# Key features by column blocks, token normalising in SBUF by GpSimd, and a reordered end, in a kernel of convolution, attention and experts

## The chip, the cores and the metric

The kernel runs on one core of a Trainium2 chip. The metric is the device time of one execution in microseconds (us). The core's engines are TensorE (PE in the profile; PEld is its loading of weights), VectorE (DVE), ScalarE (ACT), GpSimd (POOL) and SyncE (SP), which issues all DMAs of this kernel from one queue in program order. Engines run side by side and wait for each other by semaphores. All data is float32, and each matmul stands in the profile as two records.

## The reference, cut to what matters

Eight images of 128 channels and 36 x 36 positions go through two layers. The names of the inputs are shortened here.

```python
# layer 0: group norm, convolutions, an attention of 1296 queries on 34*34 keys, 1x1 convolutions
x = x + _L0_conv_ref(_gn(x), c0, w_x, ...)
# layer 1, on tokens: t is (8, 1296, 128)
t = _to_tokens(x)
t = t + _L1_attn_ref(_ln_t(t), ...)
t = t + _L1_ffn_ref(_ln_t(t), ...)

def _L1_attn_ref(x, mask, Wq, bq, Wk, bk, w, bw):
    q = einsum('bld,ed->ble', x, Wq) + bq
    k = einsum('bld,ed->ble', x, Wk) + bk
    t = tanh(q[:, :, None, :] + k[:, None, :, :])
    scores = einsum('bijd,d->bij', t, w) + bw[0]
    return einsum('bij,bjd->bid', softmax(scores), x)

def _L1_ffn_ref(x, gate_w, gate_b, weight1, weight2):   # 64 experts, the 8 best tokens of each
    probs = softmax(einsum('bsd,ed->bse', x, gate_w) + gate_b, axis=1)
    topv, topi = the 8 largest over s, for each expert
    pooled = einsum('bked,bke->bed', x at topi, topv)
    h = gelu([pooled, 1] @ weight1)          # 129 x 512 for each expert
    out = [h, 1] @ weight2                   # 513 x 128 for each expert
    return zeros with out * topv added at topi
```

The tanh of a sum, for all 1296 x 1296 pairs and 128 channels of each image, is nearly all of the work.

## The kernel before

**Scores.** The sum over 128 channels of w * tanh(q + k) is turned into quotients of sums over products: 8 blocks (`NF`) of 128 features are made of each query (`qf`, exponentials of `a_q` times the tokens) and of each key (`kf`, of `a_k`). For each slot PE makes denominators `d` and numerators `n` out of `qf` and `kf` (`products`, L903 to 916), ACT makes 1/d as exp(-ln d) (`lq`, L933 and L936), and the products n * lq are added up. In slots k = 2, 5, 8, 11 (`DVE_PAIRS`) DVE multiplies and adds (L951 to 960); in the other slots DVE multiplies into `rp` (L964, three buffers) and POOL adds (`accp`, L971 and L973). ACT takes the exponential `e` of the sum (L993). A unit is one chunk of 432 queries against one tile of 128 keys and has 12 slots; the last tile of an image has 16 keys, comes sixth (`order`, L879) and takes 2 slots. An image has 3 chunks of 11 units, and the loop of L1072 goes through all slots of all images. `denominators` runs three slots ahead of `numerators`.

**What runs beside the scores.** Everything else is written as generators in four lanes (L1026), highest first: `first_of_all` (query features, the small tile's sums), `urgent` (`attend`: softmax-weighted sum of tokens, once the 11 `e` of a chunk are there), `gates` (`gating` of the image before) and `background` (of the next image: `normal`, `conv_keys`, `layer0`, `tokens`, `keys`). Each generator yields what it wants next. `take_turns` (L1031) runs steps that want no matmul, at most one for each lane in a slot, and in a slot of `DVE_PAIRS` for `first_of_all` only. `matmul_turn` (L1036) runs a turn of matmuls after each slot's own; `background` and the others are paced by a balance that grows by 400 columns per slot (`PACE`), and get no turn in the slot before one of `DVE_PAIRS`. So the order of all engines' instructions is fixed when the program is built.

**Steps that the change touches.** `tokens` (L586) transposes the image by PE (`tpl`) to `tok`, writes that to DRAM, takes mean and variance by DVE, transposes the image a second time (`tpn`), and DVE normalises from PSUM into `xh` (L640); `xh` is transposed to `xT`. `keys` (L664) makes the key features of one tile of 128 keys in two turns of four matmuls; ACT takes one exponential of 128 x 512 for each turn (L684), and SP writes to `kd` in DRAM. `prefetch` (L887) loads a unit's features `kf` from there two units ahead. For the 16-key tile POOL writes two masked copies (L689). `attend` works through each chunk's four query tiles with 11 matmuls in two PSUM groups. `gate_logits` transposes attended tokens `t2` to `t2T`, stores that to DRAM as the residual `t2d`, transposes it back (`tp3`), and DVE normalises from PSUM (L800). `gate_tokens` takes the softmax and the 8 largest for each expert, writes them to DRAM (`gd`) and makes `pooled`.

**The end.** After the loop the score buffers are given up. Four groups of expert weights (`load_experts`: 4 experts, w1 and w2 of 1 MB each, 4 buffers for each) are loaded, the last chunk's `attend` and the last image's gating run, then SP issues all gates and residuals, and 16 groups run: `inner` (matmuls with w1, bias, gelu), `turned` (transposes) and `outer` (matmuls with w2). The loads of group 4 and on are issued in that loop. Results go through DRAM (`eod`), are multiplied by the gates, added to the residuals and written out.

Of the kernel before, what the change touches and what calls it, by code (L numbers as in the profile page):

```python
# [70 lines left out]
def kernel(  # L71
# [44 lines left out]
    kd = [dram.tile([NKT, 128, NF * 128], F32, tag=f"kd{b % 2}", name=f"kd{b}") for b in range(NB)]  # L116
# [4 lines left out]
    pooled = const.tile([128, E, NB], F32, tag="pooled", name="pooled")  # L121
# [5 lines left out]
    with ExitStack() as loop, ExitStack() as score:  # L127
# [7 lines left out]
        big = pool("big", 8, ctx)  # L135
        chunks = pool("chunks", 8)
        etp = pool("etp", NKT + 1)
# [131 lines left out]
        TAKE = (False, 1)  # L269

# [313 lines left out]
        prepared, made = {}, set()  # L584

        def tokens(b):  # L586
# [43 lines left out]
            yield matmuls(3)  # L630
            for g in range(0, NKT, 2):
                tp = aux("tpn")
                some = list(range(g, min(g + 2, NKT)))
                for t in some:
                    o, n = KT[t]
                    turned_to(tp[:n, (t - g) * C : (t - g + 1) * C], r[:, o : o + n], ident)
                yield TAKE
                for t in some:
                    n = KT[t][1]
                    nc.vector.tensor_scalar(  # L640
                        xh[:n, t, :C], tp[:n, (t - g) * C : (t - g + 1) * C],
                        mv[:n, t, 0:1], rs[:n, t : t + 1], ALU.subtract, ALU.mult,
                    )
                yield matmuls()
# [19 lines left out]
        def keys(b, tiles):  # L664

            xT = prepared[b][1]
            yield matmuls(1)
            for t in tiles:
                o, n = KT[t]
                first = (b, t) == (0, order[0])  # L670
                if first:
                    kf_of[0] = kfp.tile([128, NF, 128], F32, tag="kf", name="kf")
                for q0 in (0, NF // 2):
                    some = slice(q0, q0 + NF // 2)
                    pk = aux("pk1").rearrange("p (q t) -> p q t", t=128)
                    for q in range(NF // 2):
                        bmm(pk[:, q, :n], a_k[:, (q0 + q) * 128 : (q0 + q + 1) * 128],
                           xT[:, o : o + n], start=True, stop=True)
                    yield TAKE
                    if first:  # L680
                        ks = kf_of[0][:, some, :]
                    else:
                        ks = kstp.tile([128, NF // 2, 128], F32, tag="ks", name="ks")
                    nc.scalar.activation(ks[:, :, :n], pk[:, :, :n], AF.Exp)  # L684
                    kd3 = kd[b][t].rearrange("p (q t) -> p q t", t=128)[:, some, :]
                    if n == REM:

                        for x in range(2):
                            nc.gpsimd.tensor_scalar(  # L689
                                ks[:, :, (x + 1) * n : (x + 2) * n], ks[:, :, :n],  # L690
                                pairs[:, min(q0, 1), x : x + 1], None, ALU.mult,
                            )
                        nc.sync.dma_start(kd3[:, :, : 2 * n], ks[:, :, n : 3 * n])
                    else:
                        nc.sync.dma_start(kd3, ks)
                    if q0 > 0:
                        made.add((b, t))
                    yield matmuls()
# [15 lines left out]

        def attend(b, c, es):
# [11 lines left out]
            for i, at in enumerate(own):  # L727
                sums = two.tile([T, C + 1], F32, tag="sums", name="sums")
                for some in (range(6), range(6, NKT)):
                    pa = aux("pa1")[:T, : C + 1]  # L730
                    for j in some:
                        if j < NKT - 1:
                            e, v = es[j][:, i * T : (i + 1) * T], xh[:, j, :]
                        else:
                            rows = slice(32 * i, 32 * i + REM)
                            e, v = es[j][rows, :T], xr[rows]
                        bmm(pa, e, v, start=(j == some[0]), stop=(j == some[-1]))
                    yield TAKE
                    if j < NKT - 1:
                        nc.vector.tensor_copy(sums, pa)  # L740
                        yield matmuls()
# [21 lines left out]
        def gate_logits(b, chunks):  # L763
# [23 lines left out]
            for c in chunks:  # L787
                tp, tt = turned(c, "t2T")
                yield TAKE
                nc.vector.tensor_copy(tt, tp[:, :CH])  # L790
                nc.sync.dma_start(t2d[b][:, c * CH : (c + 1) * CH], tt)
                yield matmuls(1)
                for j0 in range(0, TPC, 2):
                    tp = aux("tp3")
                    for j in (j0, j0 + 1):
                        turned_to(tp[:T, j * C : (j + 1) * C], tt[:, j * T : (j + 1) * T], ident)
                    yield TAKE
                    for j in (j0, j0 + 1):
                        t = c * TPC + j
                        nc.vector.tensor_scalar(  # L800
                            t2[:T, t, :], tp[:T, j * C : (j + 1) * C],
                            mv[:, t, 0:1], rs[:, t - tiles[0] : t - tiles[0] + 1],
                            ALU.subtract, ALU.mult,
                        )
                    yield matmuls()
# [65 lines left out]

        def drain(*gens):
            for g in gens:
                for _ in g:
                    pass
# [11 lines left out]
        def prefetch(u):  # L887
            if u < len(units) and u not in kf_of:
# [3 lines left out]
                kf = kfp.tile([128, NF, 128], F32, tag="kf", name="kf")  # L892
                nc.sync.dma_start(
                    kf[:, :, :n], kd[b][j].rearrange("p (q t) -> p q t", t=128)[:, :, :n]
# [92 lines left out]
        def exps(p, u, d):  # L987
# [6 lines left out]
            es.setdefault((b, c), {})[j] = e  # L994
            if len(es[b, c]) == NKT:
                urgent.append(attend(b, c, es.pop((b, c))))
# [34 lines left out]
        def take_turns(p, k):  # L1031
            for lane in lanes:
                if lane.due(p, False) and (k not in DVE_PAIRS or lane is first_of_all):
                    lane.run(p)
# [25 lines left out]
        drain(tokens(0), keys(0, order[:1]))  # L1060
# [7 lines left out]
        drain(keys(0, order[1:3]))  # L1068
        prefetch(1)
        urgent.append(keys(0, order[3:]))  # L1070
        pending = deque()
        for p, (u, k) in enumerate(slots):  # L1072
            b, c, j = units[u]
            rem = j == NKT - 1
            if k == 0:
                prefetch(u + 2)
                if c == 0 and j == 1:
                    if b > 0:
                        gates.append(gating(b - 1))
                    if b + 1 < NB:  # L1080
                        background.extend(
                            (normal(b + 1), conv_keys(b + 1), layer0(b + 1), tokens(b + 1),
                             keys(b + 1, range(NKT)))
# [20 lines left out]
        while pending:  # L1104
# [7 lines left out]
            tc.tile_pool(name="wts", bufs=4, side="right", reuse_waits="tile")  # L1112
# [7 lines left out]
        def load_experts(g):  # L1120
            es = slice(g * EG, (g + 1) * EG)
            w1 = wts.tile([128, EG, HID], F32, tag="w1", name="w1")
            nc.sync.dma_start(w1, weight1[es, :128, :].rearrange("e d h -> d e h"))
# [168 lines left out]
```

## Time and profile before

| what | us |
|---|---|
| median of three runs | 6157.78 |
| lowest and highest run | 6153.82, 6159.6 |
| the profiled execution | 6152.63 |
| its span, first to last instruction | 6150.6 |
| first `e` of the scores (L993) starts | 199.5 |
| last `e` starts | 5978.4 |
| first matmul of the experts (L1165) | 6016.5 |
| last copy to `out_s` ends | 6119.8 |

Of the page, the busy shares say how long each engine had an instruction in it, the row PEclk the clock that TensorE was granted in tenths, the row GB/s what DMA moved in each of 40 slices. Granted clock of the core over the span: 0.986. In a group's line the number behind the bar is the busy time, then the mean duration of one instruction in ns, then the idle time of the engine just before them with what ended it. In views by stretch of time, busy times of each engine are given in us with the number of instructions. A chain of waits goes back from the last instruction, at each step to what released it; "issue" is time for which the profile shows no wait.

### The profile page before, as it was taken

Reading aid. Unit: us, or ns where it says so; the run is one execution under the profiler, and the core shown is the slowest. Engines: PE = TensorE matmul, PEld = TensorE weight load, DVE = VectorE, ACT = ScalarE, POOL = GpSimd, SP = SyncE. Lnnn points to the kernel's source line nnn. Section 1 sums busy time; section 2 is a strip of 40 time slices with the busy share of each in tenths; the row PEclk is TensorE's granted clock in tenths of the full one; section 3 lists DMA queues with packets and bytes.
Section 4 is the critical chain, followed back from the end, with each engine's and each line's share of the span. In section 5 each row is a group of like instructions: output and inputs, shape, how many; then the busy total and the mean of one; then the engine's idle time right before and its main releaser. Section 6 shows DMA issues by size and latency. Waiting matters only on the chain.

```text
span 6150.6 us, 93223 instructions
## 1 busy us (share of the span) xinstructions
PE 5963.4 (97%) x33576; PEld 2866.4 (47%) x33576; DVE 4798.4 (78%) x9518; ACT 5281.1 (86%) x5371; POOL 4597.5 (75%) x2804
## 2 busy tenths in 40 slices
PE   7999999999999999999999999999999999999996
PEld 5454444544544445444445444454454444544443
DVE  4787878878787787877888777887778878788872
ACT  1888898888988899888998899888898888999980
POOL 4777777777778777878687777877777777787870
PEclk9999999999999999999999999999999999999997
DMA  1200011000210001100111001100021000100017
GB/s 47 71 33 22 25 62 52 20 25 28 72 38 24 26 32 64 42 22 23 49 52 37 22 20 63 45 33 22 28 71 39 24 26 27 61 29 29 25 71 262
DMA packets 150239, 270.88 MB, mean 44 GB/s; under 512 B 45392, under 2 KB 74960, under 8 KB 149776
## 3 DMA queue, kind: packets, MB, share of 16 engines
q1 hardware_dynamic: 149776, 264.92, 12.9%
q8 instruction: 265, 4.34, 0.3%
q14 instruction: 198, 1.62, 0.1%
HBM read 200.41 MB, written 64.19 MB: 43 GB/s over the span
## 4 chain that ended last, share of the span: by engine, by line
PE 76%; ACT 8%; DVE 6%; issue 6%; POOL 2%; DMA 1%; SPq 1%; POOLq 0%; DVEq 0%; ACTq 0%
PE n L910 37%; PE d L910 12%; PE pa L281 7%; ACT lq L933 6%; PE pc L281 5%; PE s L281 3%; PE pk L281 3%; PE pq L281 3%; DVE rp L964 2%; DVE n L958 1%; DVE accd L960 1%; PE d L915 1%; ACT lq L936 1%; PE n L915 1%; ACT e L993 1%
## 5 line engine op out<-in xcount | busy, mean ns | idle before, releaser
L973 POOL TENSOR_TENSOR accp<-accp,rp 128x864 f32<-128x864 f32 x1440 | 2917.0, 2026 | 1032.0 <-DVE rp L964 938.9
L910 PE MATMUL n<-qf,kf 32*128 32x432 f32 (+1 forms) x11520 | 3320.8, 573 | 47.6 <-ACT e L993 13.3
L910 PE MATMUL d<-qf,kf 32*128 32x432 f32 (+1 forms) x11520 | 2983.8, 560 | 39.5 <-ACT lq L933 38.9
L933 ACT ACTIVATE lq<-d 128x864 f32<-128x864 f32 x2928 | 2525.3, 879 | 531.2 <-PE d L910 502.6
L964 DVE TENSOR_TENSOR rp<-n,lq 128x432 f32<-128x432 f32 x3912 | 2174.4, 600 | 739.8 <-PE d L910 539.9
L936 ACT ACTIVATE lq<-lq 128x1728 f32<-128x1728 f32 (+1 forms) x1464 | 2398.2, 1638 | 46.3
L910 PEld LDWEIGHTS n<-qf,kf 32*128 32x128 f32 (+1 forms) x11520 | 1207.1, 184 | 1603.2 <-DVE rp L964 584.0
L910 PEld LDWEIGHTS d<-qf,kf 32*128 32x128 f32 (+1 forms) x11520 | 1088.6, 185 | 420.9 <-issue 225.0
L958 DVE TENSOR_TENSOR n<-n,lq 128x432 f32<-128x432 f32 x1440 | 815.2, 608 | 138.7 <-PE n L910 83.7
L960 DVE TENSOR_TENSOR accd<-n,accd 128x432 f32<-128x432 f32 x1440 | 867.4, 602 | 24.7
L971 POOL TENSOR_TENSOR accp<-rp 128x864 f32<-128x864 f32 x240 | 485.5, 2023 | 194.7 <-DVE rp L964 192.0
L708 POOL TENSOR_SCALAR qf<-qf,cs_s 128x432 f32<-128x432 f32 x192 | 261.2, 1366 | 45.1 <-ACT qf L707 44.4
L281 PEld LDWEIGHTS pa<-xh,e 128*108 128x108 f32 x1920 | 226.1, 176 | 123.7 <-DVE rp L964 53.3
L982 POOL TENSOR_TENSOR accd<-accp,accd 128x432 f32<-128x432 f32 x240 | 265.3, 1106 | 18.8
L980 POOL TENSOR_TENSOR accp<-accp 128x432 f32<-128x432 f32 x240 | 264.6, 1103 | 16.7
L281 PE MATMUL pa<-xh,e 128*108 128x129 f32 x1920 | 265.4, 286 | 6.0 <-DVE accd L960 3.1
L281 PE MATMUL s<-q,k 128*116 128x432 f32 x480 | 230.3, 568 | 1.7 <-DVE q L313 1.4
L281 PEld LDWEIGHTS pk<-xT,a_k 128*128 128x128 f32 x1408 | 171.4, 192 | 107.0 <-DVE n L958 33.7
L459 POOL TENSOR_TENSOR tot<-tot,e 116x432 f32<-116x432 f32 x192 | 212.2, 1105 | 6.0 <-ACT e L468 4.6
L468 ACT ACTIVATE e<-s 116x432 f32<-116x432 f32 x240 | 125.0, 521 | 96.7 <-PE s L281 96.3
L281 PE MATMUL pa<-e,vw 116*128 116x432 f32 x480 | 204.6, 549 | 0.0
L281 PE MATMUL pk<-xT,a_k 128*128 128x128 f32 (+1 forms) x1408 | 202.6, 287 | 0.1
(212 smaller groups left out, 3786.5 us busy)
## 6 DMA issues: line engine op xcount, KB each, us to landing
kf<-kd SPq DMA_DIRECT2D x239, 512.0 KB
kd<-ks SPq DMA_DIRECT2D x158, 256.0 KB
w<-in_weight_dram SPq DMA_DIRECT2D x32, 1024.0 KB
wk_t<-wk_t_d SPq DMA_DIRECT2D x7, 768.0 KB
wv_t<-wv_t_d SPq DMA_DIRECT2D x7, 768.0 KB
wq_t<-wq_t_d SPq DMA_DIRECT2D x7, 768.0 KB
x<-in_x_dram SPq DMA_DIRECT2D x8, 648.0 KB
t<-tokd SPq DMA_DIRECT2D x96, 54.0 KB
```

Of the source, the lines that this page charges most:

```text
L281: mm(out, lhsT, rhs, **kw)
L708: nc.gpsimd.tensor_scalar(qf[:, 1, :], qf[:, 0, :], cs_s[:, q : q + 1], None, ALU.mult)
L910: mm(outs[h][:, :CH], kf[rows[h], q, :], qf_of[b, c, q][rows[h], part, :], start=True, stop=True)
L933: nc.scalar.activation(lq[:, o : o + n, :], d[:, :n, :CH], AF.Ln)
L936: nc.scalar.activation(some, some, AF.Exp, scale=-1.0)
L958: mult(ns[h], ns[h], lq[:, o + h, :])
L960: nc.vector.tensor_add(live["d"], ns[h], live["d"])
L964: mult(rp[:, h, :], n, lq[:, o + h, :])
L971: nc.gpsimd.tensor_add(live["p"], live["r"], rp)
L973: nc.gpsimd.tensor_add(live["p"], live["p"], rp)
L980: nc.gpsimd.tensor_add(s[:, 0, :], s[:, 0, :], s[:, 1, :])
L982: nc.gpsimd.tensor_add(d, s[:, 0, :], d)
```

## The change

- `kd` becomes [128, 8, 1296] per image. `keys` works on a block of columns, 432 wide as a rule: for each of the 8 feature blocks one matmul of 432 columns, one exponential and one DMA of 432 columns. `kf` loads take 128 columns out of each of 8 rows. The masked copies of the 16-key tile are collected in `kr` (16 small POOL operations instead of 4) and go to `krd` with one DMA. For image 0 columns 0 to 512 are made ahead of the loop (before: three tiles, 384).
- `tokens` normalises `tok` in SBUF by POOL, without the second transpose. `gate_logits` normalises `t2` in place, by POOL (by DVE for the last chunk of the last image), without `tp3`. Both yield `ASIDE`, a new kind of step that runs only in slots of `DVE_PAIRS`.
- For the last chunk of the last image, 9 of 11 tiles are attended in `attend_early` as soon as their `e` are there, into sums in SBUF; `attend` then adds the last two.
- Four residuals are loaded during the last image, the gates of seven images and one residual ahead of the last image's `gate_tokens`, gates into the buffers of `e`. The other residuals and gates follow it.
- Expert weights come in single tiles, nine buffers for w1 and w2 together, in the order in which they are used: w1 of group g ahead of w2 of group g - 2.
- `inner` adds the biases of a group with one matmul over 64 rows, with a POOL copy `which` that picks the rows, instead of four over 16 rows. `pooled` is read where it lies; the padded copy `pooled_s` goes.

```diff
+            yield ASIDE
+            for t, (o, n) in enumerate(KT):
+                nc.gpsimd.tensor_scalar(
+                    xh[:n, t, :C], tok[:n, t, :], mv[:n, t, 0:1], rs[:n, t : t + 1],
+                    ALU.subtract, ALU.mult,
+                )
+                if t % 3 == 2 or t == NKT - 1:
+                    yield ASIDE if t < NKT - 1 else step()
...
+        def keys(b, lo, hi):
...
+            for q in range(NF):
+                pk = aux("pk1")[:, :n]
+                bmm(pk, a_k[:, q * 128 : (q + 1) * 128], xT[:, lo:hi], start=True, stop=True)
+                yield TAKE
+                ks = kf_of[0][:, q, :] if first else kstp.tile(
+                    [128, CH], F32, tag="ks", name="ks")[:, :n]
+                nc.scalar.activation(ks, pk, AF.Exp)
+                nc.sync.dma_start(kd[b][:, q, lo:hi], ks)
+                if hi == N:
+                    for x in range(2):
+                        nc.gpsimd.tensor_scalar(
+                            kr[:, q, x, :], ks[:, n - REM :],
+                            pairs[:, q // (NF // 2), x : x + 1], None, ALU.mult,
+                        )
+                yield matmuls()
...
+        def attend_early(b, c, es):
+            xh, _, xr = prepared[b]
+            held = [chunk_tile("sums") for _ in range(TPC // 2)]
+            for i in range(TPC):
+                at = (i % 2) * (C + 1)
+                sums = early[i] = held[i // 2][:T, at : at + C + 1]
+                for some in (order[:5], order[6 : NKT - 2] + order[5:6]):
+                    pa = aux("pa1")[:T, : C + 1]
+                    weigh(pa, i, some, es, xh, xr)
+                    yield TAKE
...
-                yield matmuls(1)
-                for j0 in range(0, TPC, 2):
-                    tp = aux("tp3")
...
+            yield ASIDE
+            eng = nc.vector if chunks[0] == NCH - 1 else nc.gpsimd
+            for c in chunks:
+                for t in range(c * TPC, (c + 1) * TPC):
+                    eng.tensor_scalar(
+                        t2[:T, t, :], t2[:T, t, :], mv[:, t, 0:1],
+                        rs[:, t - tiles[0] : t - tiles[0] + 1], ALU.subtract, ALU.mult,
+                    )
+                yield ASIDE if c < chunks[-1] else step()
...
             for lane in lanes:
-                if lane.due(p, False) and (k not in DVE_PAIRS or lane is first_of_all):
+                if k not in DVE_PAIRS or lane is first_of_all:
+                    if lane.due(p, False):
+                        lane.run(p)
+                elif lane.due(p, None):
                     lane.run(p)
...
-        drain(keys(0, order[1:3]))
+        drain(keys(0, 128, 512))
         prefetch(1)
-        urgent.append(keys(0, order[3:]))
+        for lo, hi in ((512, 896), (N - REM, N), (896, N - REM)):
+            urgent.append(keys(0, lo, hi))
...
+                    if b == NB - 1:
+                        gates.append(residuals(4))
...
+        for g in range(NGR + 2):
+            if g < NGR:
+                to_load.append((w1s, g))
+            if g >= 2:
+                to_load.append((w2s, g - 2))
...
+        for b in range(NB - 1):
+            load_gates(b)
+        res.append(big_tile("res")[:, :N])
+        nc.sync.dma_start(res[4], t2d[4])
         drain(gate_tokens(NB - 1))
...
+        which = hidp.tile([E, EG * 32], F32, tag="which", name="which")
+        nc.gpsimd.tensor_copy(
+            which.rearrange("p (q x) -> p q x", q=EG), of_group.to_broadcast([E, EG, 32])
+        )
+        mm(ph, which, b1_s, start=True, stop=False)
         for q in range(EG):
+            o = (g * EG + q) * NB
+            mm(ph[32 * q : 32 * q + 32, :], pooled_s[:, o : o + 32], w1s[g][:, q, :],
+               start=False, stop=True)
...
-        if len(experts) < NGR and g >= 2:
-            experts.append(load_experts(len(experts)))
+        for _ in range(min(1 + (g >= 2), len(to_load))):
+            load_next()
```

## The prediction

> **What bounds the kernel now.** I read four views in this order: the page's busy shares, busy time by stretch of the loop, the chain of waits of the end, and the groups of the operations that change. The page first:
>
> ```profile
> PE 5963.4 (97%) x33576; PEld 2866.4 (47%) x33576; DVE 4798.4 (78%) x9518; ACT 5281.1 (86%) x5371; POOL 4597.5 (75%) x2804
> PEclk9999999999999999999999999999999999999997
> GB/s 47 71 33 22 25 62 52 20 25 28 72 38 24 26 32 64 42 22 23 49 52 37 22 20 63 45 33 22 28 71 39 24 26 27 61 29 29 25 71 262
> ```
>
> No engine is idle, and 97% of PE settles nothing. DMA matters in the last slice alone. Busy time by stretch (columns: length, then PE, PEld, DVE, ACT, POOL, clock, DMA share, GB/s):
>
> ```profile
> 2298.00:2323.00 25.00, 25.00 (x164) 14.18 (x156) 17.15 (x31) 24.22 (x29) 17.08 (x11) 1.00 0.31 111
> 5832.00:5852.00 20.00, 19.28 (x98) 7.68 (x96) 16.73 (x31) 19.81 (x21) 16.84 (x11) 1.00 0.08 27
> 1690.00:1712.00 22.00, 20.50 (x108) 10.13 (x107) 20.46 (x44) 18.66 (x18) 18.01 (x10) 1.00 0.10 27
> 1712.00:1734.00 22.00, 21.63 (x119) 10.44 (x118) 21.44 (x46) 20.75 (x21) 17.68 (x13) 1.00 0.07 25
> ```
>
> Row two is a unit of the last image, where nothing runs beside the scores: 12 slots take 20 us (its `e` exponentials come at 5928.45 and 5948.40), with ACT at 99%. Row one is a unit with `keys` of the next image beside it: 25 us, PE full, but ACT at 97% right behind it. Rows three and four are gating: 22 us, with PE and DVE both at 93 to 98%. POOL has 3 to 8 us free per unit. So the loop is bound by several engines at once; taking work off one of them gives only the distance to the next.
>
> The end, from the chain of waits in order of time:
>
> ```profile
> 5981.56 13.32 issue
> ...
> 6010.47 5.39 PE ppool L281 x24
> ...
> 6017.01 6.29 DMA gates<-gd
> 6023.31 14.06 DMA gates<-gd
> ...
> 6050.08 16.14 DMA w<-in_weight_dram
> ...
> 6089.55 14.48 DMA w<-in_weight_dram
> ...
> 6117.09 1.98 PE pout L1190 x32
> 6119.10 0.70 DVE out_s L1194
> ```
>
> and what DMA moved from 5900 to 6152, in 40 slices of 6.3 us:
>
> ```profile
> GB/s 0 0 122 0 0 0 3 0 0 0 3 0 334 391 387 284 4 55 113 291 300 299 275 384 387 385 387 385 387 385 387 385 387 138 0 42 43 299 415 132
> ```
>
> Scoring ends at 5973. Eight weight tiles are loaded by 6000; then DMA rests until the gate chain of the last image is through (6016), because all gates, residuals and further weights are issued behind it. From 6017 it is a DMA stage: 7.96 MB of gates and residuals until about 6041, then 24 weight tiles at 385 to 387 GB/s, one group per 5.41 us, until about 6110. Then 9.8 us of PE work to 6119.8, and 30.8 us of output to the end at 6150.6.
>
> **What the Trainium skill says.** "Trainium Kernel Development and Optimization", Performance Expectations: matmul busy time is a bad metric since matmuls are pipelined. The trace agrees: it shows PE 96% busy in the 20 us row, where PE has only its own scores, so 96% leaves far more room than 4%. "GPSIMD Engine Reference", Engine selection: two-input elementwise work is about twice as slow on GpSimd, one-input work about line-rate. The first agrees (128x432 adds: 1103 ns on L980 against 602 on L960); the second doesn't (128x128 with a scalar: 612 on L372, against 402 for DVE on L640). "TensorE: Matmul & The Clock Gate", Why this matters for your kernels: idle gaps over about 3 us drop PE to half clock. The trace agrees: after 13.25 us of waiting, at 6050, eight `phid` matmuls take 1.93 us instead of 1.06. "DMA: Bandwidth & Descriptors", Specifications: at least 512 B for line-rate; the new `kf` loads are in pieces of just that size. No view here prices them singly. The same table's 358 GB/s from HBM is exceeded: 387.
>
> **Part by part.** Groups used (count | busy us, mean ns):
>
> ```profile
> L684 ACT ACTIVATE ks<-pk 128x512 f32<-128x512 f32 x158 | 92.4, 587 | 1.2 <-PE d L910 1.2
> L640 DVE TENSOR_SCALAR xh<-tpn,ln_mv,ln_rs 128x128 f32<-128x128 f32 x80 | 28.5, 402 | 3.0 <-POOL ln_rs L262 2.3 <-PE tpn L285 0.7
> L800 DVE TENSOR_SCALAR t<-tp,t_mv,t_rs 108x128 f32<-108x128 f32 x96 | 34.6, 402 | 7.3 <-POOL t_rs L262 7.3
> L372 POOL TENSOR_SCALAR wxn<-w_x,gn_rs 128x128 f32<-128x128 f32 x8 | 4.9, 612 | 0.8
> ```
>
> *Keys by blocks.* Per image 22 turns become 24. A turn of four 128-column matmuls (eight records) holds PE 1.09 us in the timeline (2303.04 to 2304.13): 20 full turns and two short ones, about 23.5 us. A 432-column matmul is two records 0.36 us apart (as L910's), so 0.83 with the change-over, times 24 = 19.9. PE gains 3.6 us. ACT: 20 x 587 + 2 x 207 = 12.2 us becomes 24 x 519 (line through these two sizes) = 12.5. As ACT leaves only 0.78 us in 25, over three such units PE's relief is worth at most 2.3 us; I take 1.5. The `kr` masks go from 4 x 446 ns to 16 at some 335 (estimate from the 446 at 64 columns and 612 at 128): 3.6 us more on POOL, in the unit where `qf` already has it at 27.1 of 29.0 us; I charge 0.5, bounds 0 and 3.
>
> DMA: 24 `kd` writes for 22 and `kf` loads in 1024 pieces of 512 B instead of 128 of 4 KB stand in SP's queue. A `kf` load is issued two units, 40 to 50 us, ahead; a load of 512 KB takes 1.4 us at 387 GB/s, so even at a third of that rate it is hidden: 0. Were it not, every unit would wait, some 3 us each.
>
> *Normalising by GpSimd.* Removed per image: 11 + 12 transposes and 23 x 402 ns = 9.2 us of DVE. Added: 23 x 612 = 14.1 us of POOL, in DVE_PAIRS slots, where POOL gets no product. A group of three takes 1.84 us, behind it wait the next `accp` additions, and for those DVE's `rp` (three buffers). One 2.03 us addition and 1.84 fit two slots of 3.3 us only nearly. In gating the stretch of 44 us has POOL at 35.7; with 7.3 more it is 43.0. So of the 4 us above the quiet 40 I take 1 (bounds -2 and 3.5). For tokens, POOL has 12 us free of 46, but the phase shows little excess: 0.5 (bounds -3 and 1.5).
>
> Loop per image: 1.5 - 0.5 + 1 + 0.5 = 2.5 us, times 7 = 17 us.
>
> *Start.* Nothing hides tokens of image 0: 11 x 612 = 6.7 us replaces DVE's 3.59 (142.05 to 145.64), +3; and `keys` to column 512 before the loop instead of 384, +2. Sum +5.
>
> *attend_early.* In the last image a chunk's attend costs (25.9 + 21.0) - 2 x 20.0 = 6.9 us between `e`s for 44 matmuls; 36 of them inside the last two units cost 5 us. The gate chain after the last `e` gets some 9 us shorter (13.32 us wait above), but isn't what ends last.
>
> *The end's DMA,* from 5976: nine tiles 24.4 us at 387 GB/s, biases and `t2d` 1.3, seven gates in the former idle time 9 (2.3 MB at 257 GB/s, my split of the mixed stretch), one residual 1.7, the last gate out 1.3, one residual 1.7, a wait of SP for that gate's or the tile's release 2, two residuals and the last gate in 4.7, 23 tiles 62.3: 6084.5, landed by 6086. Weights come in order of use, so after the last one only one `outer` and a copy remain: 2.8 us, 6088.9 against 6119.8: 31 us. Less 5 for the later start (attend_early) and 1 for PE at half clock: 25, bounds 15 and 33. Four residuals earlier cost nothing: DMA is at 5 to 10% there. The smaller bias matmul and no `pooled_s` copy lie under DMA.
>
> Sum: -25 - 17 + 5 = -37 on the run's 6152.6 (span 6150.6 plus 2 around it): 6115. The median shown is 5 us higher, so 6120.
>
> **Rivals.** (B) ACT and POOL take all of the loop's gain: -20, 6138. For it: ACT 97%, POOL 43 of 44. Against: DVE and PE both get lighter in gating. (C) Everything taken off counts: keys and tokens stand at 14.8 us above the quiet pattern per image (last five intervals of an image, 24.6 23.0 25.3 26.1 24.5, against 23.9 20.0 20.0 22.8 22.0), gating at 4.4; eight of these go: -56 instead of -17, 6081. Against: ACT keeps its work. (D) Slower: POOL becomes the bound. If a one-input operation takes 1.1 us beside DVE instead of 0.61, 25 us per image meet the 13 us that seven groups find free; 12 us reach DVE through `rp`, 4 are gained back: 8 x 7 = 56 more, less the 20: 6194. It decides from about 0.85 us each. Against: L708's 128x432 takes 1366 ns under the same load. (E) The end doesn't do what it says: SP sits in order behind a slow release, the weights resume late, the end gives 8: 6137.
>
> **How the numbers follow.** Forecast A 0.45, B 0.15, C 0.18, D 0.11, E 0.11. Likeliest 6120, its own range 6100 to 6137. For 8 in 10: 6080 (C) to 6155. This measurement can't tell less than 0.2% (12 us) from no change. Faster is A, C and most of B and E: 0.82; same 0.07; slower D: 0.11.
>
> **What would show it.** `pk` with 384 records of 432 columns, mostly, and units beside keys at 24 to 25 us still with ACT over 96%; no `tpn`; L640's successor on POOL at 0.6 to 0.7 us; gating units near 21.5; the first `e` some 5 us after 199.5; weights resuming within 5 us of the last gate; last weight to `out_s` under 4 us. I'm wrong if POOL's operation is over 0.85 us, if units beside keys fall to 22, or if DMA rests over 6 us in the end.

## The result, and the profile after

The changed kernel takes 6209.8 us in the median of four runs (6206.3 to 6211.6), the kernel before 6155.8 beside it: a ratio of 1.0090, with a 95% interval of 1.0077 to 1.0103. It is slower by 0.9% where 0.6% faster was forecast. The profiled execution has a span of 6206.3 us. Cut at the first exponential `e` of each image, the time went here (us; the last column is the difference):

| part | before | after | |
|---|---|---|---|
| start, to the first `e` | 199.5 | 210.4 | +10.9 |
| image 0 | 742.2 | 750.3 | +8.1 |
| images 1 to 6, each | 735.9 | 742.7 | +6.9, six times: +41.1 |
| last image, first to last `e` | 621.5 | 639.4 | +17.9 |
| end, last `e` to the last instruction | 172.2 | 149.9 | -22.3 |

So the end did most of what it was to do, and the loop lost three times that. The page's totals hardly show it (busy us, share of the span, instructions; then the granted clock):

```profile
PE 5962.1 (96%) x32304; PEld 2760.6 (44%) x32304; DVE 4751.0 (77%) x9341; ACT 5282.7 (85%) x5403; POOL 4756.1 (77%) x3095
PEclk9999999999999999999999999999999999999997
```

POOL has 159 us more to do, DVE 47 less; PE's loading of weights fell from 47% to 44%, and no other share moved by more than 2 points. Stretches show more (columns as in the prediction; rows: a unit beside `keys`, a quiet unit of the last image, two units of gating of image 2, and a unit of the last image with gating of one chunk):

```profile
2322.22:2346.15 23.93, 23.79 (x111) 8.94 (x110) 17.46 (x32) 23.17 (x28) 16.36 (x10) 1.00 0.26 87
6003.03:6022.97 19.94, 19.23 (x108) 8.25 (x106) 17.01 (x32) 19.75 (x20) 16.32 (x10) 1.00 0.01 1
1723.92:1748.86 24.94, 21.55 (x105) 9.40 (x103) 17.74 (x37) 19.97 (x20) 24.52 (x23) 0.89 0.04 6
1748.86:1771.70 22.84, 22.84 (x122) 10.14 (x120) 21.55 (x44) 20.42 (x20) 22.29 (x19) 0.97 0.09 24
5663.24:5691.00 27.76, 25.86 (x117) 9.88 (x117) 19.14 (x36) 19.99 (x21) 19.47 (x12) 0.84 0.03 6
```

The first two rows are as good as before or better. In gating POOL went from 18 busy us to 24.5 of 24.9, the granted clock from 1.00 to 0.89, and the unit of 22 us takes 24.9. Of the first four units of image 2 the first is shorter than before, 21.2 us for 23.3, and the next three are longer: 24.9 for 21.9, 22.8 for 20.6, 19.2 for 17.1. The last row is a unit that takes 20 us when nothing runs beside it. The operations that the prediction priced (count | busy, mean ns | idle before):

```profile
L819 POOL TENSOR_SCALAR t<-t,t_mv,t_rs 108x128 f32<-108x128 f32 x92 | 71.8, 792 | 0.0
L637 POOL TENSOR_SCALAR xh<-tok,ln_mv,ln_rs 128x128 f32<-128x128 f32 x80 | 62.6, 795 | 0.0
L684 POOL TENSOR_SCALAR kr<-ks,pairs 128x16 f32<-128x16 f32 x128 | 39.9, 327 | 15.4 <-DVE rp L993 8.2 <-ACT ks L679 7.2
L679 ACT ACTIVATE ks<-pk 128x432 f32<-128x432 f32 x168 | 87.1, 519 | 0.0
```

POOL's normalising takes 792 to 795 ns, where 612 was assumed from an operation with one scalar; this one has two. The exponential and the masks came out as priced. Before, DVE hardly waited for POOL's additions to free an `rp`; now it does (who waited for whom; us in all, times, longest; the kernel before, then the changed one):

```profile
DVE rp L964 <- POOL accp L971: 6.9, 5, 1.9
DVE rp L993 <- POOL accp L1000: 58.8, 26, 4.2
```

How operations of 0.8 us lead to such waits, the timeline of image 2 shows (start us, duration, engine, line, operation; in brackets the idle time before it and what ended it):

```profile
1731.64 0.15 DVE L261 TENSOR_SCALAR ve<-pgv 128x1 f32<-128x1 f32 x1
...
1734.39 3.13 POOL L819 TENSOR_SCALAR t<-t,t_mv,t_rs 108x128 f32<-108x128 f32 x4
...
1739.73 2.01 POOL L1000 TENSOR_TENSOR accp<-rp 128x864 f32<-128x864 f32 x1
1741.72 3.12 POOL L819 TENSOR_SCALAR t<-t,t_mv,t_rs 108x128 f32<-108x128 f32 x4
1741.77 1.12 DVE L993 TENSOR_TENSOR rp<-n,lq 128x432 f32<-128x432 f32 x2 [4.16 <-POOL accp L1000]
1742.43 0.59 PE L290 MATMUL tp<-ident,t 108*128 108x108 f32 x4 [2.59 <-DVE rp L993]
1744.81 0.57 POOL L266 TENSOR_TENSOR gn_rs<-ve,neg_half 128x1 f32<-128x1 f32 x1
1745.48 0.61 POOL L377 TENSOR_SCALAR wxn<-w_x,gn_rs 128x128 f32<-128x128 f32 x1
1746.06 12.50 POOL L1002 TENSOR_TENSOR accp<-accp,rp 128x864 f32<-128x864 f32 x6
1746.39 0.89 ACT L962 ACTIVATE lq<-d 128x864 f32<-128x864 f32 x1 [4.36 <-PE d L939]
```

POOL works through its queue in order. Groups of four (`t`) stand ahead of its additions, the three `rp` buffers stay full, DVE stops for 4.16 us, PE for 2.59 behind DVE, ACT for 4.36 behind PE. Then POOL works through six additions in a row. In the same queue stands `wxn`, a small step of the next image: its input `ve` is there at 1731.8, it starts at 1745.5. The granted clock over the whole span fell from 0.986 to 0.980 beside these stops; no run here tells what the clock costs by itself.

The end, from the chain of waits and from what DMA moved between 5956 and 6208:

```profile
6056.42 7.20 issue
...
6104.05 9.06 DMA w<-in_weight_dram
6113.24 1.93 PE pout L1250 x32
...
6152.75 14.51 DMA w<-in_weight_dram
```

```profile
GB/s 0 3 83 0 1 121 0 0 0 4 0 0 3 0 1 62 396 386 387 360 156 173 277 262 349 387 386 386 388 385 387 387 385 376 33 42 44 258 398 188
```

A slice is 6.3 us. DMA no longer rests: weights flow from 6055 on, and in between the gates and residuals move at 156 to 277 GB/s. The wait that ends at 6167.3 isn't for the last weight tile: PE has the `outer` of two more groups to do after it, and weight data moves until 6172.2, 115.7 us after the last `e`. The first seven gates are the slow part (columns as above):

```profile
6080.40:6094.00 13.60, 12.88 (x51) 6.37 (x54) 0.96 (x2) 0.60 (x1) 0.57 (x2) 0.50 0.68 179
```

### The profile page after: what moved, and what is told of

The parts are those of the page before. It is cut to its first block, busy times and chain, and to the rows that moved or that the text cites. A ratio compares the mean times of both kernels' runs of the same rounds, so it can differ in the third digit from the quotient of the medians.

```text
span 6206.3 us, 90994 instructions
## 1 busy us (share of the span) xinstructions
PE 5962.1 (96%) x32304; PEld 2760.6 (44%) x32304; DVE 4751.0 (77%) x9341; ACT 5282.7 (85%) x5403; POOL 4756.1 (77%) x3095
## 4 chain that ended last, share of the span: by engine, by line
PE 72%; ACT 7%; DVE 7%; POOL 6%; issue 6%; DMA 1%; SPq 0%; POOLq 0%; DVEq 0%; ACTq 0%
PE n L939 35%; PE d L939 12%; PE pa L286 7%; PE pc L286 5%; ACT lq L962 5%; PE s L286 3%; DVE rp L993 3%; PE pk L286 2%; POOL accp L1002 2%; PE pq L286 2%; DVE n L987 1%; PE d L944 1%; DMA w<-in_weight_dram 1%; POOL accp L1000 1%; PE n L944 1%
## 5 line engine op out<-in xcount | busy, mean ns | idle before, releaser
L939 PE MATMUL n<-qf,kf 32*128 32x432 f32 (+1 forms) x11520 | 3355.2, 576 | 61.0 <-DVE rp L993 19.8
L939 PEld LDWEIGHTS n<-qf,kf 32*128 32x128 f32 (+1 forms) x11520 | 1223.4, 185 | 1757.3 <-DVE rp L993 687.2
L982 DVE TENSOR_TENSOR accd<-n,lq 128x432 f32<-128x432 f32 x240 | 144.6, 603 | 75.0 <-ACT lq L965 46.7
L286 PE MATMUL pk<-xT,a_k 128*128 128x432 f32 (+3 forms) x416 | 192.5, 554 | 2.3 <-ACT ks L679 2.3
```

The source lines that it names most:

```text
L286: mm(out, lhsT, rhs, **kw)
L939: mm(outs[h][:, :CH], kf[rows[h], q, :], qf_of[b, c, q][rows[h], part, :], start=True, stop=True)
```

## The experiments

Each is an edit of the changed kernel unless it says otherwise. The ratio is to the kernel before, run beside it.

**Gating put back.** POOL's operations on `t2` go, the second transposes and VectorE's operations return.

```diff
-                    eng.tensor_scalar(
-                        t2[:T, t, :], t2[:T, t, :], mv[:, t, 0:1],
...
+                        nc.vector.tensor_scalar(
+                            t2[:T, t, :], tp[:T, j * C : (j + 1) * C],
```

> The changed kernel with the gating part alone put back as it was before: t2 is transposed a second time from t2T and normalised by VectorE out of PSUM; tokens, keys by blocks, the end and the early attend stay as changed. Theory T (POOL's normalising of t2 holds up the loop, by its order or by its load): the 8.7 us that image 2 loses in its first stretch (245.2 against 236.5) go, times seven images 61, and the two 27.8 us units of the last image go back to 20 to 23, another 10 to 15: 6130 to 6145 instead of 6210. Theory K (keys by blocks is what costs): the time stays within 12 us of 6210, and the first stretch of an image stays near 245.

6161.4 us, 1.0013 (1.0007 to 1.0020): 48 us come back. Images 1 to 6 take 737.4 instead of 742.7, the last 624.8 instead of 639.4. This is the part that cost most. It is 16 us above the theory's range, since without it the rest of the change doesn't gain in the loop: images 1 to 6 took 735.9 before.

**Tokens put back.** The same for `xh`.

```diff
-                nc.gpsimd.tensor_scalar(
-                    xh[:n, t, :C], tok[:n, t, :], mv[:n, t, 0:1], rs[:n, t : t + 1],
...
+                    nc.vector.tensor_scalar(
+                        xh[:n, t, :C], tp[:n, (t - g) * C : (t - g + 1) * C],
```

> The changed kernel with the token part alone put back: a second transpose from the channel-major map and VectorE's normalising out of PSUM. In the trace the stretch with tokens lost nothing (253.8 against 253.7), and the start lost 11 us of which some 5 are POOL's eleven operations with nothing beside them. Theory T-gating (only gating's POOL work costs): 6200 to 6210, the gain being the start's 3 to 6 us. Theory T-load (POOL is simply overloaded wherever normalising runs): a second loss of some 5 us an image lies in the stretch with tokens too, 6165 to 6180.

6207.9, 1.0091 (1.0077 to 1.0104): no more than 2 us. Inside it the start is 6.9 us shorter (203.5), images 1 to 6 are 1.6 us longer each.

**Later transposes.** Tests whether PE merely comes too early to POOL's tiles.

```diff
-                yield ASIDE if c < chunks[-1] else step()
+                yield ASIDE if c < chunks[-1] else step(8)
...
-                    yield ASIDE if t < NKT - 1 else step()
+                    yield ASIDE if t < NKT - 1 else step(8)
```

> The changed kernel, with the same operations on the same engines, but the transposes of the normalised tiles come eight slots (some 14 us) after the last group was handed to POOL instead of one, in gating and in tokens. Theory O (order: PE comes to these transposes before POOL is through and everything behind them on PE waits): POOL's load is unchanged but no longer met in order, so most of the 61 + 15 us comes back: 6140 to 6165, and PE's wait for POOL's t before the transposes falls from 2 to 3 us to under 0.5. Theory L (load: POOL's 23 x 0.79 = 18 us per image delay its accp additions, DVE's rp waits for them, wherever the transposes stand): 6195 to 6215, with DVE's wait on accp near its 58.8 us in all.

6232.6, 1.0129 (1.0115 to 1.0143): slower still, by 23 us. DVE's wait for `accp` stays at 57.8 us. My first theory, the order, fell. Outside the last image the trace of the changed kernel has no wait of PE for `t`, so there was nothing to gain. (In the last image the eight slots have no effect, as `exps`, L1019, drains the urgent lane at once when a chunk's second `e` comes; there PE does wait for `t` itself, 7.5 us in all.) What costs the 23 us wasn't traced in full; PE's waits before `pb` (below) grow from 1.9 to 12.2 us.

**VectorE, SBUF to SBUF.**

```diff
-            eng = nc.vector if chunks[0] == NCH - 1 else nc.gpsimd
+            eng = nc.vector
...
-                nc.gpsimd.tensor_scalar(
+                nc.vector.tensor_scalar(
                     xh[:n, t, :C], tok[:n, t, :], mv[:n, t, 0:1], rs[:n, t : t + 1],
```

> The changed kernel with both normalisings still from SBUF to SBUF and in the same places in the order, but on VectorE instead of POOL. 23 operations an image leave POOL (18 us) and come to DVE (some 23 x 0.25 to 0.4 us, under what it had before with PSUM as a source). Theory P (POOL is the cause, by order or load): 6120 to 6140, below before, since the second transposes stay away. Theory K (keys by blocks is what costs): 6195 to 6215. Theory D (the place among VectorE's product slots costs whichever engine does it, since a group of four comes ahead of products): in between, 6160 to 6180.

6314.2, 1.0262 (1.0248 to 1.0276): far above all three. VectorE's groups:

```profile
L637 DVE TENSOR_SCALAR xh<-tok,ln_mv,ln_rs 128x128 f32<-128x128 f32 x80 | 87.0, 1139 | 2.4 <-POOL ln_rs L266 2.3
L819 DVE TENSOR_SCALAR t<-t,t_mv,t_rs 108x128 f32<-108x128 f32 x96 | 82.4, 918 | 0.6 <-POOL t_rs L266 0.6
```

918 and 1139 ns on the engine that took 402 out of PSUM. Taken one by one, 90 of the 184 take 0.33 to 0.35 us, as at the start, where POOL rests; the other 94 take 0.85 to 2.2 us, and each of these ends 78 to 89 ns after an operation of POOL's, mostly an addition. So this run doesn't settle the question it was made for; see the last section.

**Smaller groups.** Six groups of two instead of three of four.

```diff
-                yield ASIDE if c < chunks[-1] else step()
+                    if t % 2 == 1:
+                        yield ASIDE if (c, t) != (chunks[-1], c * TPC + TPC - 1) else step()
```

> The changed kernel with gating's twelve normalising operations handed to POOL in six groups of two, one group at each of VectorE's product slots, instead of three groups of four. Same operations, same engines, same POOL time. Theory L (load: 9.5 us more on POOL in a stretch where it was already short of time): the loss stays, 6200 to 6220, and DVE's wait for POOL's accp additions stays near the 58.8 us of the changed kernel. Theory B (burst: a group of 3.1 us is longer than what two slots leave, a group of 1.6 us isn't): most of gating's 48 us comes back, 6165 to 6180, and the waits on accp fall below 30 us.

6258.6, 1.0176 (1.0162 to 1.0190): 49 us slower than with groups of four. The theory of bursts as I had put it fell: spread out, the same operations meet the window copies of the next image on POOL (`xwin`, L398 to 402), and in each of six images one wait of DVE for POOL is 5.8 to 5.9 us long.

**Keys put back,** with the layout of `kd` and the loads of `kf`.

```diff
-            for q in range(NF):
-                pk = aux("pk1")[:, :n]
...
+                for q0 in (0, NF // 2):
+                    some = slice(q0, q0 + NF // 2)
+                    pk = aux("pk1").rearrange("p (q t) -> p q t", t=128)
```

> The changed kernel with the keys alone put back: four 128-column matmuls and one exponential per half of a key tile, masks of the last tile in ks. With gating undone, 9 us were left at the first e, 8 in image 0 and 1.5 in each further image against before, and tokens explain 7 of the start and -1 per image. Theory K (keys by blocks cost a little: wider turns, 16 small masks for POOL, more to do before the loop): 6180 to 6192. Theory N (keys neutral): 6204 to 6215. Forecast of the prediction (keys a gain of 1 per image and a start cost of 2): 6213 to 6217.

6207.8, 1.0093 (1.0079 to 1.0107), as the neutral theory had it, but by two effects that cancel: image 0 is 9.4 us shorter without the change (740.9), the start 2.0; images 1 to 6 are 2.1 us longer each (744.8).

**The end alone.** The three edits that put gating, tokens and keys back, together.

> Keys, tokens and gating as before; of the change only the end and the early attend of the last chunk are kept. Theory S (the parts add up): 6153 of before, less the 22.3 us measured between the last e and the end, plus 3.4 us for the early attend in the last image: 6132 to 6138. Theory I (the end's gain needs something of the other parts, such as POOL's earlier t2): 6145 to 6155.

6137.3, 0.9980 (0.9973 to 0.9986), as the theory of the sum said. From the last `e` to the last instruction 149.2 us.

**The end without the early attend.** On top of the one just told:

```diff
-            if (b, c) == (NB - 1, NCH - 1) and len(es[b, c]) == NKT - 2:
-                urgent.append(attend_early(b, c, es[b, c]))
```

> As the kernel with only the end kept, but without the early attend: all of the last chunk's attend stands behind the last e again. Theory G (the last gate ends later and the queue of weights waits behind it): the last image is 3.4 us shorter, the end 5 to 10 longer: 6134 to 6144, above the one with the early attend by 2 to 7. Theory F (the gate chain is hidden under the weights): 6128 to 6134, below it by 3.4.

6134.8, 0.9975 (0.9966 to 0.9984). The last image is 3.9 us shorter (621.7), and the end is no longer, 148.2: the gate chain lies under the weights. The early attend brings nothing that these runs can tell: the two times are 2.5 us apart.

**Useless work for POOL.** Gating put back on VectorE, and POOL does its twelve operations again, into a scratch buffer.

```diff
+            if chunks[0] == 0 and len(chunks) == NCH:
+                yield ASIDE
+                scratch = chunk_tile("scratch")
...
+                        nc.gpsimd.tensor_scalar(
+                            scratch[:T, :C], t2[:T, t, :], mv[:, t, 0:1],
```

> The kernel with gating undone, in which VectorE normalises t2 out of PSUM, plus gating's twelve POOL operations again, on the same tiles and at the same product slots in groups of four, but into a scratch buffer that no instruction reads. It does useless work and leaves the output as it is. Without that work it took 6161 us. Theory L (POOL's 9.5 us in the gating stretch are the cost, whoever reads the result): 6195 to 6225. Theory W (PE's transposes waiting for POOL's result are the cost): 6161 to 6170.

6255.5, 1.0167 (1.0153 to 1.0181), 94 us over the kernel without the scratch work, and above my range. Nobody reads these results, so it isn't the wait for them; it is what stands behind them in POOL's queue: DVE's waits for POOL's additions grow from 30.2 to 70.6 us. That the cost is twice gating's 48 us isn't explained; here VectorE keeps its own work, and the scratch tile takes a buffer of `chunks`.

**Four `rp` buffers,** and the control with three.

```diff
-        chunks = pool("chunks", 8)
+        chunks = pool("chunks", 7)
-        kstp = pool("kstp", 3, score, "right")
+        kstp = pool("kstp", 2, score, "right")
-        rpp = pool("rpp", 3, score, "right")
+        rpp = pool("rpp", 4, score, "right")
```

> The changed kernel with four rp buffers between VectorE's products and POOL's additions instead of three, room being made by seven chunk buffers instead of eight and two ks buffers instead of three. Theory Q (POOL's backlog comes in bursts and stops VectorE because three rp buffers are soon full): DVE's wait for accp falls from 59 us to under 30, time 6170 to 6195. Theory M (POOL is short of time on average over the gating stretch, so a buffer more only puts the stop off): 6203 to 6215, or more if a scarcer chunk or ks buffer costs something.

> The changed kernel with seven chunk buffers instead of eight and two ks buffers instead of three, but three rp buffers as before: the control to the kernel with four. Theory Q (the fourth rp buffer made the 52 us): 6205 to 6225. Theory R (the smaller rings moved the order of work and that made it): 6155 to 6180.

With four 6157.5, 1.0008 (0.9999 to 1.0016); with three and the same smaller rings 6219.4, 1.0107 (1.0093 to 1.0121). The buffer is worth 62 us, more than theory Q had, with POOL's load unchanged; the theory of rings (the sets of buffers used in turn) is out. The wait that it takes away, from the waits view of the control (us in all, times, longest):

```profile
DVE rp L993 <- POOL accp L1000: 67.5, 29, 4.5
```

With four 7.1 us are left of all DVE's waits for POOL's additions. So POOL isn't short of time on average. But another wait comes up: PE before `pb`, for `wxn`, 27.8 us where it was 1.9.

**Four `rp` buffers where POOL doesn't normalise:** the same three lines, in the kernel with the end alone and no early attend.

> Keys, tokens and gating as before, the end as changed without the early attend (6134.8 us), with four rp buffers, seven chunk and two ks buffers. Theory P (the fourth buffer takes up POOL's backlog, and only POOL's normalising makes a backlog; in the kernel before DVE waits 6.9 us for accp in all): 6126 to 6142. Theory E (a fourth rp buffer is worth tens of us in any of these kernels): 6085 to 6115.

6099.4, 0.9912 (0.9899 to 0.9926): 35 us, as theory E had it. In that kernel three buffers show another wait, `rp` for `rem`, the matmuls of the 16-key tile that hold the buffers: 22.1 us, 24 times. It goes too, and those units fall from 7.9 us to 6.3 and 6.0. In the traces, counted between the `e`, the units of the 16-key tile make 35.3 of the 41.1 us gained here, and 30.5 of the 56.4 gained above. So some 30 to 35 of the 62 us have nothing to do with POOL's normalising. That the other 26 or so have is a difference between kernels that are not alike in all else: this pair has no control with the smaller rings, and above keys and tokens are changed too.

**Tokens, then keys as well, for images 1 to 7,** on the end alone without early attend, image 0 as before. The edits of tokens and of keys are made for `b > 0` only:

```diff
+            if b == 0:
...
+                        nc.vector.tensor_scalar(
...
+            else:
...
+                    nc.gpsimd.tensor_scalar(
```

> Keys and gating as before, the end as changed without the early attend, and POOL's normalising of tokens for images 1 to 7 only; image 0 keeps VectorE's, out of PSUM. Base is the kernel with the end alone and no early attend, 6134.8. From the kernels with and without the tokens' part, images 1 to 7 gain some 1.2 us each and image 0's start loses 7: theory A (that holds without the other parts too) 6124 to 6131; theory B (POOL has no room there either once keys are as before) 6134 to 6145.

> As the kernel with the end and the tokens of images 1 to 7, plus keys by blocks for images 1 to 7, while image 0 keeps the tile-by-tile keys. The masks of the last tile go into the free columns of ks, with one small transfer each. The traces with and without the keys' part gave a gain of 2.1 us for each later image and a loss of 9 for image 0. Theory A: 6110 to 6119. Theory B (the gain of keys in later images was the alignment of one order and does not carry over): 6124 to 6135.

6157.7, 1.0007 (0.9999 to 1.0016), and 6137.9, 0.9977 (0.9968 to 0.9986), both above all my ranges. Images 1 to 6 take 736.8 with neither, 738.9 with tokens, 737.6 with both. (The traced run with tokens is the fastest of its 13, 8 us under the median, so it shows less than the usual loss.) Tokens on POOL lose 2.1 us an image here and gained 1.6 in the changed kernel: their sign hangs on what else stands around them.

**What is left with four buffers.** The changed kernel with four `rp`, image 0 as before, no early attend; and then its gating transposes four slots later:

```diff
-                yield ASIDE if c < chunks[-1] else step()
+                yield ASIDE if c < chunks[-1] else step(4)
```

> The changed kernel with four rp buffers (6157.5), less what it loses elsewhere: image 0's tokens are normalised by VectorE out of PSUM (7 us of start), image 0's keys tile by tile (2 us of start and 9 in the image), and no early attend (2.5). The parts add up: 6132 to 6142. They don't, as with tokens and keys in the kernel of the end alone: 6145 to 6160.

> As the kernel before it in this list, with gating's transposes of POOL's tiles four slots after the last group instead of one. Theory O2 (with four rp buffers the order does count: PE stands before these transposes until POOL's t is there, ACT idles 3 to 4 us each time): 5 to 30 us faster than that kernel. Theory L2 (what is left is POOL's load): no faster, 0 to 20 us slower.

6141.5, 0.9980 (0.9972 to 0.9988), where the parts add up, and 6161.5, 1.0013 (1.0007 to 1.0020). Order fell a second time; again PE waits for `t` in the last image alone. But the timeline of the first names another reader of POOL's queue:

```profile
1711.14 0.15 DVE L261 TENSOR_SCALAR ve<-pgv 128x1 f32<-128x1 f32 x1
...
1721.24 3.12 POOL L868 TENSOR_SCALAR t<-t,t_mv,t_rs 108x128 f32<-108x128 f32 x4
1724.33 0.57 POOL L266 TENSOR_TENSOR gn_rs<-ve,neg_half 128x1 f32<-128x1 f32 x1
1725.00 0.61 POOL L377 TENSOR_SCALAR wxn<-w_x,gn_rs 128x128 f32<-128x128 f32 x1
1725.67 0.59 PE L286 MATMUL pb<-gm,wxn 128*128 128x1 f32 x2 [4.33 <-POOL wxn L377]
```

`wxn` of the next image starts 13.9 us after its input, and PE stands before `pb` for 4.33 us, with the scores behind it; seven such waits make 27.9 us in this run, and 34.1 in the one with later transposes. Before the change `wxn` started after 5.0 us (`ve` at 1721.83, `wxn` at 1726.80).

**Room in front of `pb`.** One number in `normal`, on top of the kernel just shown:

```diff
-            yield matmuls(3)
+            yield matmuls(10)
             pb = aux("pb")
```

> The kernel with four rp buffers and image 0 as before (x15, 6141.5 us), with one number changed: PE's matmul pb, which needs the next image's wxn from POOL, comes ten slots after wxn was handed to POOL instead of three. In the trace of x15 wxn stands behind twelve of gating's operations and the additions between them, ve being ready at 1711.1 and wxn at 1725.6, and PE waits 4.3 us in front of pb, with everything of the loop behind it. Theory V (what is left of gating's loss is this second reader of POOL's queue, PE standing in front of pb): 6105 to 6130. Theory L2 (what is left is POOL's load in general, the stop only moves): 6138 to 6155.

6097.5, 0.9910 (0.9895 to 0.9924): 44 us, more than the theory had. The waits before `pb` fall from 27.9 to 1.9 us; the rest isn't divided, and the edit also puts all later steps of `normal` seven slots later. In the kernels where VectorE normalises PE waits 1.9 us in all before `pb`, so there is nothing of this wait to gain there. In image 2 `wxn` is there at 1714.5 and `pb` comes at

```profile
1726.72 0.38 PE L286 MATMUL pb<-gm,wxn 128*128 128x1 f32 x2
```

with nothing of POOL in front of it. In the second unit of image 2 POOL is busy for 20.25 of 20.49 us, and the unit isn't longer for it (21.9 us in the next kernel):

```profile
1692.28:1712.77 20.49, 19.70 (x109) 9.28 (x105) 18.42 (x37) 19.88 (x21) 20.25 (x19) 1.00 0.05 8
```

Images 1 to 6 take 731.2 us, within 0.5 of the next kernel (730.8), in which VectorE does gating and tokens: POOL's 0.79 us operations then cost next to nothing there. The last image keeps its loss, 625.6 us for 612.9: two units there still take 27.7 and 27.5 us, with PE waiting for `t`.

**Keys alone, with four buffers:** the keys' edit for `b > 0`, on the kernel with the end and four `rp`.

> The kernel with the end and four rp buffers (x14, 6099.4 us), plus keys by blocks for images 1 to 7, image 0 tile by tile; tokens and gating as before. Theory A (keys by blocks gain 2 us per later image where POOL has room): 6083 to 6092. Theory B (they gain nothing, as the kernel with tokens and keys and the one with neither, 6138 and 6135, say): 6096 to 6106.

6090.3, 0.9899 (0.9883 to 0.9916): keys by blocks gain 1.6 us per later image (730.8 against 732.4). It is the fastest of all, 61 us under the kernel before: the end without early attend, keys by blocks from image 1 on, four `rp` buffers.

## Why the prediction was wrong

The sum was -37, measured was +55.7 of the span. Where the 93 us lie:

| step | forecast | measured |
|---|---|---|
| keys, images 1 to 6 | gain 1 each | gain 2.1, 1.3 and 1.6 in three pairs |
| tokens, images 1 to 6 | gain 0.5 each | gain 1.6 or loss 2.1, by what is around |
| gating, images 1 to 6 | gain 1 each | loss 5.3 each (742.7 against 737.4) |
| image 0 beside this | none | +8.1; keys alone 9.4 |
| start | +5 | +10.9; tokens 6.9, keys 2.0, 3.3 with the end alone |
| early attend | +5 | +4 |
| gating by chunks in the last image | none | +14.6 (639.4 against 624.8) |
| end | -31 and +1 | -22.3 |

**The step that failed** is this one: "In gating the stretch of 44 us has POOL at 35.7; with 7.3 more it is 43.0. So of the 4 us above the quiet 40 I take 1". It has a wrong size, 0.79 us for 0.61, but that isn't the failure: with 0.79 the mean would have said 45.2 us of work in 44, so that it doesn't fit; yet with one buffer more and a later `pb` it does, and the loss is gone from images 1 to 6 (731.2 us each). The failure is to hold a mean busy time against a stretch, for an engine that works in order and has two readers with little slack. In the changed kernel DVE stops, having three `rp` buffers (58.8 us of waits for 6.9 before). Once it has four, PE stops, having three slots before `pb` (27.8 us for 1.9). The sentence before it, "One 2.03 us addition and 1.84 fit two slots of 3.3 us only nearly", saw the queue and then left it for the mean. I never asked what else stands in POOL's queue at that time; `wxn` and the window copies were in the trace of before.

**Rival D** named the direction, and the road by `rp` to DVE; its time, 6194, is the nearest. Its cause and its threshold don't hold: it made POOL the bound by its load from 0.85 us on, and the loss was there at 0.79, and gone at 0.79, outside the last image, with another buffer and another slot.

**Keys** were right for the loop: units beside them take 23.9 us, ACT at 97%, as the forecast had them. Missed was image 0, where the blocks run urgently beside the first units (30.0 us for 25.8). The masks were put at 335 ns; a line through the two sizes that the prediction names gives some 322, and 327 came. **Start:** eleven of POOL's operations took 8.5 us instead of 6.7, and the transposes of `xT` wait for them one by one. The 3.3 us in the kernel with the end alone were not traced to a cause.

**End.** The DMA sum was too small: from the first weight data to the last it has 108.5 us (5976 to 6084.5), and 117.0 passed (6055.2 to 6172.2). The gates and residuals in between took 26.8 us (6080.2 to 6107) where 21.7 were counted, as the first seven gates went at 179 GB/s and not at 257; the last 23 tiles took 65.2 for 62.3. The tail held: "only one `outer` and a copy remain: 2.8 us", and 3.2 us passed until `out_s` (6175.4). The cost of the early attend was priced well (3.9 us in the last image for 5), and the end is no shorter for it.

## What to carry to other kernels

Before work goes to an engine with free time, list what stands behind it in that engine's own queue at that place, who reads each of those results, and how many buffers or slots that reader has in hand. A mean busy time of 81% says nothing on a burst of 3 us in front of a result that is needed in 2. And where such a move loses, a deeper ring or a later reader may be the cure, rather than its undoing.

## What the runs showed of the hardware

VectorE's normalising takes 402 ns out of PSUM, 330 to 350 ns out of SBUF with POOL at rest, and up to 2.2 us out of SBUF when one of POOL's additions runs. The Trainium skill, "SBUF — State Buffer", Who interferes with whom, gives a reason: VectorE's `tensor_scalar` from SBUF to SBUF can take a second pair of ports that is GpSimd's only one, and the one that comes second is blocked until the first is through. The case agrees: all 94 slow ones end within 0.1 us after the end of an operation of POOL's, while POOL's additions keep their 2.02 us. Out of PSUM, in the kernel before, all 184 take 390 to 411 ns, the 42 that lie wholly inside one of POOL's additions too; what looked like a needless transpose had this use. Not expected either: three `rp` buffers cost 35 us without any normalising on POOL, with 22 us of waits under the name of `rem`, and only 7 under POOL's.
